# Layer 0's experts: the ScalarE gates of a block declared independent of the VectorE products of the same block

## The chip, the cores and the metric

The kernel runs on one core of a Trainium2 chip. The metric is the device time of one execution in microseconds (us), and the median of several runs is compared. Five engines work side by side, each through its own queue of instructions in order: PE (TensorE, matrix products; PEld is its loading of stationary operands), DVE (VectorE, elementwise work and reductions), ACT (ScalarE, activation functions), POOL (GpSimd, here mostly the issue of indirect transfers) and SP (SyncE, which issues the other transfers). A wait at the head of a queue holds all that stands behind it.

## The reference, cut to what matters

The program is a stack of four layers, each of attention followed by a mixture of experts, on `x` of 4 x 512 tokens with 128 features. The change lies in layer 0's experts, which compute for every token and expert

```python
h = jnp.einsum('td,edh->eth', xf, W0) + b0[:, None, :]
g = jax.nn.silu(jnp.einsum('td,edh->eth', xf, W1) + b1[:, None, :])
y = jnp.einsum('eth,ehd->etd', h * g, W2) + b2[:, None, :]
out = jnp.einsum('te,etd->td', combine.reshape(n * s, NUM_EXPERTS), y)
```

There are 8 experts with 512 hidden units, and `combine` is zero but for two experts of each token. In the code below `g` is "the gate" and `h * g` "the product".

## The kernel before, in words

The tokens are handled in two halves of 1024. `route` finds the two experts of each token and scatters the token's row into a buffer in DRAM, sorted by expert (`buf`, by POOL, L721). `experts` then works through 23 blocks of 128 sorted rows for each half of layer 0 (46 blocks), each with one expert's weights:

- `load` fetches four blocks' rows (L838, SP queue); `tokens` transposes them on PE (L848) and copies them out of PSUM.
- `up(j)` reads the expert's number, issues the load of 516 KB of weights `w` (L864, SP; three buffers) and does eight products on PE (L875) into `sc`, a PSUM tile of two banks with two buffers: the four gate chunks of 128 hidden units go to bank 1 first, and the four plain chunks to bank 0.
- `down(j)` goes over the four chunks. For each, ACT makes the gate `eg` from bank 1 (L890; four buffers), and DVE makes the product `hT` from bank 0 and the gate (L891; three buffers of four chunks). Both also read their biases from `w`, so that `w` is free for the load of block j + 3 only after the fourth product. Four products on PE follow (L902, into `av`), a copy `ys` on DVE (L910), and a store to `ybuf` (L911, SP). Two row transfers that are due, scatters or gathers, are issued on POOL behind each `ys` copy (`row_transfers`).

`down(j - 1)` is called after `up(j)`. When the first half's blocks are stored, `gather` fetches each token's two rows (`yg`, L935, POOL), two transfers behind each of the next eight `ys` copies, while the second half's blocks run; `combine` adds them to `x` on DVE (L953), and the statistics for the next layer's norm follow (L224, L226).

Nobody writes the order of layer 0 out by hand: a scheduler lays the instructions of each engine in an order that it finds with a timeline of its own, and then puts in the waits that the recorded dependencies need. Only the attention of layers 1 to 3 has a fixed order. The scheduler records a dependency between two instructions of different engines that touch the same tile in PSUM, also where both only read: so a gate of chunk `fc` on ACT waits for the product of chunk `fc - 1` on DVE, although the one reads bank 1 of `sc` and the other bank 0. The product needs the gate of its own chunk in any case.

Of the kernel before, what the change touches and what calls it, by code (L numbers as in the profile page):

```python
# [13 lines left out]
AF = mybir.ActivationFunctionType  # L14
ALU = mybir.AluOpType
# [4 lines left out]
P = 128  # L20
# [26 lines left out]
def tile_xattn_moe_stack(ctx: ExitStack, tc: tile.TileContext, a: dict, out: bass.AP):  # L47
# [10 lines left out]
    nc = tc.nc  # L58
# [13 lines left out]
    def ps_sc():  # L72
        return ps2.tile([P, 2, 512], F32, tag="sc", name="sc")

    def ps_tr():
        return ps2.tile([P, 512], F32, tag="tr", name="tr")

    def ps_av():
        return ps2.tile([P, 512], F32, tag="av", name="av")
# [3 lines left out]
    def evac(o, i, scale=None):  # L83

        turn[0] += 1
        if turn[0] % 2:
            if scale is None:
                nc.vector.tensor_copy(o, i)
            else:
                nc.vector.tensor_scalar(o, i, scale, None, ALU.mult)  # L90
        elif scale is None:
            nc.scalar.copy(o, i)
        else:
            nc.scalar.activation(o, i, AF.Copy, scale=scale)
# [545 lines left out]
    def row_transfers(n=2 * NH, behind=None):  # L640

        for start in rows_due[:n]:
            ins = start()
            if behind is not None:
                wait_for(ins, (behind,), "spread over the work beside it")
        del rows_due[:n]
# [161 lines left out]
    def wait_for(ins, others, why):  # L808
        for other in others:
            tc.add_manual_dep(  # L810
                ins.ins,
                other.ins.name,
                mybir.DependencyInfo(mybir.DependencyClass.Sync, mybir.DependencyReason.DATA),
                reason=why,
            )
# [8 lines left out]
    def experts(layer, half, routed, w2):  # L824

        ebs, _, scatters = routed
        nj, nf, nu = BLK[layer == 1], NF[layer], UPS[layer]
        pack = a[f"up{layer}"]
        width = pack.shape[2]
        bias = nu * nf * P  # L830
        loaded, toks = {}, {}

        def load(g):
            m = min(4, nj - 4 * g)
            if m <= 0:
                return
            tok = wff.tile([P, 4, D], F32, tag="tok", name="tok", bufs=2)
            get = nc.sync.dma_start(  # L838
                tok[:, 0:m, :], buf[half][4 * g * P : (4 * g + m) * P, :].rearrange("(c p) d -> p c d", p=P)
            )  # L840
            wait_for(get, scatters, "any token may lie in these blocks")
            loaded[g] = m, tok

        def tokens(g):
            m, tok = loaded.pop(g)
            q = ps_tr()
            for c in range(m):
                nc.tensor.transpose(q[:, c * P : (c + 1) * P], tok[:, c, :], ident)  # L848
            tokT = wff.tile([P, 4 * P], F32, tag="tokT", name="tokT", bufs=2)
            evac(tokT[:, 0 : m * P], q[:, 0 : m * P])  # L850
            toks[g] = tokT

        def up(j):

            xT = toks[j // 4][:, (j % 4) * P : (j % 4 + 1) * P]
            e = nc.values_load(
                ebs[0:1, j : j + 1],
                engines=[mybir.EngineType.SP, mybir.EngineType.PE],
                min_val=0,
                max_val=E - 1,  # L860
                skip_runtime_bounds_check_because="a count of at most E - 1, by a minimum",
            )
            w = wff.tile([P, 1032], F32, tag="w", name="w")
            nc.sync.dma_start(w[:, 0:width], pack[bass.ds(e, 1), :, :].rearrange("o p n -> p (o n)"))  # L864
            sc = ps_sc()
            for u in reversed(range(nu)):
                for fc in range(nf):
                    at = (u * nf + fc) * P
                    if layer == 0:
                        dst = sc[:, u, fc * P : (fc + 1) * P]  # L870
                    elif layer == 3:
                        dst = sc[:, fc // 2, fc % 2 * P : (fc % 2 + 1) * P]
                    else:
                        dst = sc[:, 0, fc * P : (fc + 1) * P]
                    nc.tensor.matmul(dst, w[:, at : at + P], xT, start=True, stop=True)  # L875
            return e, w, sc

        stores = []

        def down(j, e, w, sc):  # L880
            hT = p3.tile([P, nf, P], F32, tag="hT", name="hT")
            if layer == 2:
                nc.scalar.activation(hT.rearrange("p f t -> p (f t)"), sc[:, 0, 0 : nf * P], AF.Gelu)
            for fc in range(nf if layer != 2 else 0):
                up = sc[:, 0, fc * P : (fc + 1) * P]
                b0 = w[:, bias + fc : bias + fc + 1]
                if layer == 0:
                    g = p2.tile([P, P], F32, tag="eg", name="eg", bufs=4)
                    b1 = w[:, bias + nf + fc : bias + nf + fc + 1]
                    nc.scalar.activation(g, sc[:, 1, fc * P : (fc + 1) * P], AF.Silu, bias=b1)  # L890
                    nc.vector.scalar_tensor_tensor(hT[:, fc, :], up, b0, g, ALU.add, ALU.mult)  # L891
                elif layer == 1:
                    nc.scalar.activation(hT[:, fc, :], up, AF.Gelu, bias=b0)
                else:
                    up = sc[:, fc // 2, fc % 2 * P : (fc % 2 + 1) * P]
                    if fc < 2:
                        nc.vector.tensor_scalar(hT[:, fc, :], up, b0, 0.0, ALU.add, ALU.max)
                    else:
                        nc.scalar.activation(hT[:, fc, :], up, AF.Relu, bias=b0)
            y = ps_av()  # L900
            for fc in range(nf):
                nc.tensor.matmul(  # L902
                    y[:, 0:D],
                    hT[:, fc, :],
                    w2[:, bass.ds(e, 1), fc, :].rearrange("p o d -> p (o d)"),
                    start=(fc == 0),
                    stop=(fc == nf - 1),
                )
            ys = p3.tile([P, D], F32, tag="ys", name="ys")
            row_transfers(2, nc.vector.tensor_copy(ys, y[:, 0:D]))  # L910
            stores.append(nc.sync.dma_start(ybuf[half][j * P : (j + 1) * P, :], ys))  # L911


        load(0)
        load(1)
        tokens(0)
        last = None
        for j in range(nj):
            this = (j, *up(j))
            if last:  # L920
                down(*last)
            last = this
            if j % 4 == 2 and j // 4 + 1 in loaded:
                tokens(j // 4 + 1)
                load(j // 4 + 2)
            yield
        down(*last)
        return stores

# [288 lines left out]
    gates = []  # L1218
# [176 lines left out]
```

## Time and profile before

| | us |
|---|---|
| median of three runs | 1413.1 (1406.45 to 1416.71) |
| the profiled execution | 1326.58 |
| its span, first to last instruction | 1324.7 |
| layer 0's first `up` product to its last gate | 117.85 to 293.66 |

So the profiled execution is 86.5 us shorter than the median, and 1.9 us of it lie around the span. Its mean granted TensorE clock was 0.93 of full speed; for the other runs no clock is known. The second section of the page slices the span in forty pieces of 33.1 us; layer 0's blocks fill the slices four to nine:

```profile
PE   4885897897777778988999999857899999899881
...
PEclk8786998998899889989999999988999999999996
...
GB/s 220 0 61 98 163 225 179 171 156 80 26 9 37 38 62 50 151 148 93 42 38 46 49 50 102 127 144 140 132 62 34 50 34 33 83 91 163 202 184 57
```

A digit is a busy share in tenths; GB/s is what the DMA engines moved in each slice. The two groups of instructions that the change touches, from the fifth section (count, busy time, mean ns of one, and the idle time of the engine just before them):

```profile
L890 ACT ACTIVATE eg<-sc,w 128x128 f32<-128x128 f32 x184 | 66.2, 367 | 98.5 <-DVE hT L891 72.7
...
L891 DVE SCALAR_TENSOR_TENSOR hT<-sc,w,eg 128x128 f32<-128x128 f32 x184 | 63.0, 348 | 55.1 <-ACT eg L890 52.7
```

### The profile page before, as it was taken

Reading aid. Unit: us, or ns where it says so; the run is one execution under the profiler, and the core shown is the slowest. Engines: PE = TensorE matmul, PEld = TensorE weight load, DVE = VectorE, ACT = ScalarE, POOL = GpSimd, SP = SyncE. Lnnn points to the kernel's source line nnn. Section 1 sums busy time; section 2 is a strip of 40 time slices with the busy share of each in tenths; the row PEclk is TensorE's granted clock in tenths of the full one; section 3 lists DMA queues with packets and bytes.
Section 4 is the critical chain, followed back from the end, with each engine's and each line's share of the span. In section 5 each row is a group of like instructions: output and inputs, shape, how many; then the busy total and the mean of one; then the engine's idle time right before and its main releaser. Section 6 shows DMA issues by size and latency. Waiting matters only on the chain.

```text
span 1324.7 us, 26947 instructions
## 1 busy us (share of the span) xinstructions
PE 1099.2 (83%) x9435; PEld 904.1 (68%) x9435; DVE 748.5 (57%) x2057; ACT 588.2 (44%) x2290; POOL 252.4 (19%) x281
## 2 busy tenths in 40 slices
PE   4885897897777778988999999857899999899881
PEld 3774887773343445877787778746778887789781
DVE  5572554656767566433666766424376676646452
ACT  1112443355444444536556655322565665533230
POOL 2023122204000020221000004045030000403424
PEclk8786998998899889989999999988999999999996
DMA  7013575552101121553112223444421211335762
GB/s 220 0 61 98 163 225 179 171 156 80 26 9 37 38 62 50 151 148 93 42 38 46 49 50 102 127 144 140 132 62 34 50 34 33 83 91 163 202 184 57
DMA packets 136996, 126.82 MB, mean 96 GB/s; under 512 B 13466, under 2 KB 116511, under 8 KB 136479
## 3 DMA queue, kind: packets, MB, share of 16 engines
q1 hardware_dynamic: 129695, 110.39, 30.0%
q0 software_dynamic: 7168, 14.69, 3.8%
q8 instruction: 78, 1.28, 0.4%
q14 instruction: 55, 0.45, 0.1%
HBM read 101.31 MB, written 23.72 MB: 94 GB/s over the span
## 4 chain that ended last, share of the span: by engine, by line
PE 38%; DVE 7%; DMA 6%; ACT 3%; issue 3%; POOL 2%; SPq 1%; POOLq 0%; DVEq 0%; ACTq 0%
PE sc L608 5%; PE sc L875 5%; PE tr L368 5%; PE tr L422 4%; PE av L405 4%; PE av L902 4%; DMA w<-in_up 4%; PE sc L593 2%; PE av L387 2%; ACT probs L305 2%; DVE nm L291 2%; POOL yg L935 1%; PE sc L557 1%; PE tr L848 1%; DVE aT L412 1%
## 5 line engine op out<-in xcount | busy, mean ns | idle before, releaser
L305 ACT ACTIVATE probs<-sc,nm 128x154 f32<-128x154 f32 x768 | 286.3, 402 | 169.1 <-DVE nm L291 169.0
L875 PE MATMUL sc<-tokT,w 128*128 128x128 f32 x1528 | 210.8, 287 | 32.8 <-DMA w<-in_up 26.7
L875 PEld LDWEIGHTS sc<-tokT,w 128*128 128x128 f32 x1528 | 189.7, 198 | 46.6 <-DMA w<-in_up 13.0
L291 DVE TENSOR_REDUCE nm<-sc 128x6 f32<-128x924 f32 x144 | 143.2, 1011 | 86.6 <-PE sc L608 50.7
L902 PE MATMUL av<-w,hT 128*128 x1160 | 173.4, 284 | 10.1 <-DVE hT L891 7.3
L305 ACT ACTIVATION_READ_ACCUMULATOR probs<-sc,nm 128x1 f32 x768 | 168.2, 219 | 0.0
L902 PEld LDWEIGHTS av<-w,hT 128*128 128x128 f32 x1160 | 149.9, 195 | 21.2 <-DVE hT L891 11.4
L935 POOL DMA_INDIRECT yg<-ybuf,su x112 | 106.7, 953 | 275.6 <-DVE pT L261 63.7
L233 POOL TENSOR_TENSOR rstd<-ve,nhalf 128x4 f32<-128x4 f32 x32 | 33.2, 1039 | 619.4 <-DVE ve L231 499.2
L721 POOL DMA_INDIRECT buf<-xn,su x112 | 108.1, 965 | 171.3 <-DVE hT L891 43.7
L261 DVE COPY pT<-tr 128x512 f32<-128x512 f32 x160 | 107.4, 688 | 49.2 <-PE tr L368 43.9
L368 PE MATMUL tr<-ident,probs 128*128 128x128 f32 x768 | 121.5, 289 | 0.8 <-DVE rT L334 0.6
L405 PE MATMUL av<-pT,vm 128*64 128x128 f32 (+1 forms) x1536 | 102.7, 284 | 8.8 <-DVE pT L261 8.7
L890 ACT ACTIVATE eg<-sc,w 128x128 f32<-128x128 f32 x184 | 66.2, 367 | 98.5 <-DVE hT L891 72.7
L368 PEld LDWEIGHTS tr<-ident,probs 128*128 128x128 f32 x768 | 86.0, 145 | 28.8 <-issue 12.7
L891 DVE SCALAR_TENSOR_TENSOR hT<-sc,w,eg 128x128 f32<-128x128 f32 x184 | 63.0, 348 | 55.1 <-ACT eg L890 52.7
L910 DVE COPY ys<-av 128x128 f32<-128x128 f32 x168 | 48.5, 289 | 78.7 <-PE av L902 73.3
L405 PEld LDWEIGHTS av<-pT,vm 128*64 128x64 f32 (+1 forms) x1536 | 65.3, 127 | 35.6 <-issue 18.2
L608 PE MATMUL sc<-kT,qT 64*128 64x154 f32 x1024 | 86.5, 308 | 3.5 <-ACT probs L305 3.5
L608 PEld LDWEIGHTS sc<-kT,qT 64*128 64x128 f32 x1024 | 71.0, 189 | 14.3 <-issue 9.7
L593 PE MATMUL sc<-xnT,wq 128*128 128x128 f32 x512 | 67.1, 286 | 2.9 <-ACT probs L305 2.9
L422 PE MATMUL tr<-wo,aT 128*128 128x128 f32 x512 | 66.1, 284 | 1.6 <-DVE xnT L253 1.3
(252 smaller groups left out, 1477.7 us busy)
## 6 DMA issues: line engine op xcount, KB each, us to landing
w<-in_up SPq DMA_DIRECT2D x46, 516.0 KB
w<-in_up SPq DMA_DIRECT2D x76, 258.0 KB
rep<-rd SPq DMA_DIRECT2D x64, 256.0 KB
ybuf<-ys SPq DMA_DIRECT2D x168, 64.0 KB
tok<-buf SPq DMA_DIRECT2D x36, 256.0 KB
w<-in_down SPq DMA_DIRECT2D x3, 2048.0 KB
w<-in_up SPq DMA_DIRECT2D x46, 128.0 KB
buf<-zero SPq DMA_DIRECT2D x2, 1472.0 KB
```

The lines of the kernel that those rows point to most:

```text
L261: return nc.vector.tensor_copy(o, i)
L291: nc.vector.tensor_reduce(self.at.heads(self.nm, g, n), self.sc[g][:, :, 0 : n * S2].rearrange("p j (s k) -> p j s k", s=n), AX.X, ALU.max ...
L305: nc.scalar.activation(self.pr[:, h, :], self.sc[g][:, j, s * S2 : (s + 1) * S2], AF.Exp, bias=self.nm[:, h : h + 1], accum_out=self.rs[:, ...
L368: nc.tensor.transpose(q[:, t * P : (t + 1) * P], self.pr[:, h, 0:P], ident)
L405: nc.tensor.matmul(av[rows, cols], v, self.pT[n][:, t, :], start=False, stop=last)
L422: nc.tensor.matmul(o[:, 0:D], self.aT[:, c, :], self.at.wo[:, c, :], start=(c == 0), stop=(c == self.nb - 1))
L593: nc.tensor.matmul(sc[:, c // 4, c % 4 * P : (c % 4 + 1) * P], wq[:, c * P : (c + 1) * P], at.xnT[:, i * P : (i + 1) * P], start=True, sto ...
L608: nc.tensor.matmul(sc[:, j, s * S2 : (s + 1) * S2], at.qT[i][rows, c, :], at.kT[rows, c, :], start=True, stop=True)
L721: ins = nc.gpsimd.indirect_dma_start(out=buf[half], out_offset=bass.IndirectOffsetOnAxis(ap=su[:, t : t + 1], axis=0), in_=xns[t // NI][:, ...
L875: nc.tensor.matmul(dst, w[:, at : at + P], xT, start=True, stop=True)
L902: nc.tensor.matmul(y[:, 0:D], hT[:, fc, :], w2[:, bass.ds(e, 1), fc, :].rearrange("p o d -> p (o d)"), start=(fc == 0), stop=(fc == nf - 1),)
L935: ins = nc.gpsimd.indirect_dma_start(out=yg[:, t, :], out_offset=None, in_=ybuf[half], in_offset=bass.IndirectOffsetOnAxis(ap=su[:, t : t ...
```

## The change

The products of a block are collected in a list, and each gate is declared independent of all products of its own block that come before it. Nothing is computed in another way, and no instruction is added or taken away.

```diff
         def down(j, e, w, sc):
             hT = p3.tile([P, nf, P], F32, tag="hT", name="hT")
+            products = []
...
                 if layer == 0:
                     g = p2.tile([P, P], F32, tag="eg", name="eg", bufs=4)
                     b1 = w[:, bias + nf + fc : bias + nf + fc + 1]
-                    nc.scalar.activation(g, sc[:, 1, fc * P : (fc + 1) * P], AF.Silu, bias=b1)
-                    nc.vector.scalar_tensor_tensor(hT[:, fc, :], up, b0, g, ALU.add, ALU.mult)
+                    silu = nc.scalar.activation(g, sc[:, 1, fc * P : (fc + 1) * P], AF.Silu, bias=b1)
+
+                    for other in products:
+                        tc.declare_no_dep(silu.ins, other.ins, reason="distinct banks and gates")
+                    products.append(nc.vector.scalar_tensor_tensor(hT[:, fc, :], up, b0, g, ALU.add, ALU.mult))
```

The scheduler sees other dependencies and so lays out another order. Both programs hold the same instructions on every engine. Their orders agree from the start of the program to layer 0's first blocks, and again from the start of layer 1's attention on, but for one exchange of two neighbours on DVE and one read of an expert's number that stands a few instructions further ahead on PE; in layer 0's experts they differ on all five engines. Write gate j, product j, `ys` j, D j (the four products of L902) and U j (the eight of L875) for block j, counted from 0. On DVE the order around one block in the second half's gather was and is

```text
before:  ys 23, product 24 b c d, product 25 a, combine 1a, ys 24, product 25 b, combine 1b, ...
after:   ys 23, product 24 c d, product 25 a b, ys 24, product 25 c d, combine 1a 1b, ..., product 26 a b, ys 25, ...
```

where the gathers of pair 1 (a and b: the rows of a token's two experts) are issued behind `ys` 23, those of pair 2 behind `ys` 24, and so on. On POOL one `pow` of the norm (L233) is two gathers later than it was. On PE, U j + 1 stands ahead of D j in both, and the transposes of L848 and of the route stand elsewhere among them. On SP, weight load j stands behind the store of block j - 4 before, and behind that of block j - 4 or j - 5 now.

## The prediction

> **What bounds the kernel now.** I read the busy shares of the page first, then the stretches of layer 0's experts with the busy time of each engine, then the waits inside that stage, and last the instructions in order of time.
>
> ```profile
> PE 1099.2 (83%) x9435; PEld 904.1 (68%) x9435; DVE 748.5 (57%) x2057; ACT 588.2 (44%) x2290; POOL 252.4 (19%) x281
> ```
>
> PE leads over the whole span, so ACT and DVE, the two engines that the change sets free of each other, matter only where PE waits for them. The stretches of the stage (us and count of PE, PEld, DVE, ACT and POOL, then PE's granted clock, DMA share and GB/s):
>
> ```profile
> 118.00:150.00 32.00, 28.17 (x230) 27.20 (x231) 17.46 (x74) 15.60 (x35) 0.00 (x0) 0.93 0.53 156
> 150.00:187.00 37.00, 35.60 (x287) 34.00 (x287) 19.94 (x58) 17.23 (x47) 15.38 (x16) 0.97 0.65 195
> 187.00:220.00 33.00, 26.24 (x215) 24.60 (x215) 15.18 (x47) 12.35 (x35) 3.94 (x4) 1.00 0.65 199
> 220.00:250.00 30.00, 25.25 (x171) 22.75 (x172) 17.48 (x65) 9.32 (x26) 12.61 (x13) 0.89 0.54 159
> 250.00:294.00 44.00, 40.62 (x318) 36.57 (x316) 24.45 (x75) 20.49 (x56) 1.04 (x1) 1.00 0.55 166
> ```
>
> PE is busy for 155.9 of 176 us. So 20.1 us of idle PE is nearly all that any change of this stage can win, plus what a slowed clock cost: it was 0.89 in the fourth stretch, and 0.66 in 222 to 232 us. The waits of the stage (total us, times, longest):
>
> ```profile
> ACT eg L890 <- DVE hT L891: 72.7, 130, 4.1
> DVE hT L891 <- ACT eg L890: 52.7, 97, 4.3
> ...
> DVE x L953 <- DMA yg<-ybuf,su: 11.6, 10, 3.3
> ...
> PE sc L875 <- DMA w<-in_up: 8.5, 7, 2.6
> ...
> PE av L902 <- DVE hT L891: 7.3, 11, 2.0
> ```
>
> The two largest are the ping-pong that the change cuts, 125 us; PE's own, 8.5 and 7.3 us, are small. In order of time a block of the second stretch reads (start, us, then what it waited for):
>
> ```profile
> 158.65 0.37 ACT L890 ACTIVATE eg<-sc,w 128x128 f32<-128x128 f32 x1 [0.42 <-DVE hT L891]
> 159.05 0.35 DVE L891 SCALAR_TENSOR_TENSOR hT<-sc,w,eg 128x128 f32<-128x128 f32 x1 [0.43 <-ACT eg L890]
> ...
> 159.44 0.37 ACT L890 ACTIVATE eg<-sc,w 128x128 f32<-128x128 f32 x1 [0.42 <-DVE hT L891]
> 159.79 0.97 PEld L902 LDWEIGHTS av<-w,hT 128*128 128x128 f32 x8
> ...
> 161.42 1.86 PEld L875 LDWEIGHTS sc<-tokT,w 128*128 128x128 f32 x16 [0.66 <-ACT eg L890]
> 161.45 2.02 PE L875 MATMUL sc<-tokT,w 128*128 128x128 f32 x16 [0.49 <-DMA w<-in_up]
> ```
>
> Gates follow each other at 0.79 us, one product in between. A block has three such steps and then about 0.4 us, as the next block's first gate waits for no product: 2.8 us. PE needs 1.86 + 0.97 us for U and D and 0.12 us for transposes (four in 0.47 us, every fourth block): 2.95 us. The ping-pong is thus no longer than PE's own block; it costs only because it ends late, and holds the release of `w` with it.
>
> In the second half's gather another chain rules (DVE and POOL alone):
>
> ```profile
> 213.09 0.35 DVE L891 SCALAR_TENSOR_TENSOR hT<-sc,w,eg 128x128 f32<-128x128 f32 x1 [0.38 <-ACT eg L890]
> 216.72 0.35 DVE L953 SCALAR_TENSOR_TENSOR x<-yg,wa,x 128x128 f32<-128x128 f32 x1 [3.28 <-DMA yg<-ybuf,su]
> 216.99 0.28 DVE L910 COPY ys<-av 128x128 f32<-128x128 f32 x1
> ...
> 223.38 0.35 DVE L953 SCALAR_TENSOR_TENSOR x<-yg,wb,x 128x128 f32<-128x128 f32 x1 [2.67 <-DMA yg<-ybuf,su]
> ```
> ```profile
> 217.54 1.06 POOL L935 DMA_INDIRECT yg<-ybuf,su  x1 [3.02 <-DVE hT L891]
> 218.91 0.94 POOL L935 DMA_INDIRECT yg<-ybuf,su  x1 [0.30 <-issue]
> ```
>
> A `ys` copy releases two gathers, DVE stops at the combine of these rows, and the next `ys` stands behind it: one trip of a gather for each block.
>
> **The Trainium skill.** PSUM — Partial Sum Buffer, section "PSUM bank collisions raise a hardware error", says that two engines must be kept apart by bank and quadrant, reads against reads included, and that other banks run clean. Gates and products read different banks, so running them together should cost neither of them time; nothing in this trace shows a collision. The same page, "Engine vs sequencer instructions", calls the queues of ScalarE and VectorE strict FIFO: the trace agrees, the combine's 3.28 us hold products that could have run. TensorE: Matmul & The Clock Gate, section "What's actually happening", says that the clock is halved after an idle window of about 3.4 us; the trace agrees roughly: sixteen products from 226.21 us on, after PE gaps of 1.4 and 2.0 us at 217.6 and 224.1, took 3.68 us and not 1.95.
>
> **The change part by part.** I cut the stage by the starts of `ys` copies: `ys` 0 at 126.22, 7 at 155.24, 16 at 184.57, 23 at 210.44, 32 at 251.74, 45 at 294.99 us.
>
> *Ping-pong.* 138 waits of a gate go. A gate still waits for the product that used its buffer four gates earlier, in the block before, normally long done. Two gates in a row took 0.62 to 0.87 us, so four take 1.2 to 1.6 us, and the fourth product ends some 1.8 us after U j, not 3.1. The time on ACT and DVE is hidden by PE's 2.95 us and gives nothing; what counts is the next item.
>
> *Weight loads.* Load j + 3 goes out with product j, now 1.3 us sooner. One load took 3.9 us (issued 157.50, U at 161.45), beside a token load 5.7 us (141.95 to 147.66). From product j (1.8 us after U j) to U j + 3 lie three D and two U less 1.8: 3 x 0.97 + 2 x 1.87 - 1.8 = 4.85 us. So the usual load is hidden, and one beside tokens is late by up to 0.9 us. SP's queue doesn't hold them: the store ahead of load j + 3 is that of block j - 1 or older, whose `ys` comes before product j.
>
> *126 to 155:* 29.0 us. PE needs 7 x 2.95 and 3.4 for the route's products, 24.1. The route's table loads on ACT (1.28 + 0.2 + 1.28) remain, now after gate 4 and not after gate 3a. The 2.62 us for `w` at 147.66 go, with the slow clock behind it: **3** of 4.9.
>
> *155 to 185:* 29.3 us against 9 x 2.95 + 1.9 = 28.5: **0.5**. The route's slots are ready at product 8 and not 4 of DVE, but the scatters stay behind `ys` 7 to 14: nothing.
>
> *185 to 210:* 25.9 us against 20.7. PE waited 1.55 and 2.40 us for `w` where token loads crowd (DMA share 0.94 in 187 to 192). These loads stay: **2.5**, bounds 0 and 4.
>
> *210 to 252:* 41.3 us for nine blocks, 4.6 each, against 26.6. Now the `ys` of the next block stands ahead of the combine, so two blocks share one trip: 0.55 us to the first gather, 1.37 to the second, which lands after 2.9 (median; 4.5 longest), then about 1.9 us of combine, statistics, two products and waits to the second `ys` after it: 6.7 to 8.3 us for two blocks, 3.4 to 4.2 each. Nine blocks take 30 to 37 us. I take 33.3: **8**, bounds 4 and 11. DVE still stops at combines, but with products already handed over. The `pow` that moves past two gathers on POOL costs nothing: its norm is due blocks later.
>
> *252 to 295:* 43.3 us against 13 x 2.95 and 3.3 for attention's first products, 41.7: **1**.
>
> The sum is 15 us, bounds 4 and 22 (no more than PE's idle time and its slow clock hold): 1326.6 - 15 = 1311.6 in an execution like the profiled one. The median of 1413.1 is 86.5 us above it; with a slower PE the ping-pong matters less and the gather's trip the same. I take the same 15 us off: **1398**.
>
> **The rivals.** *PE hides it* (0.37): the second and fifth stretch have PE busy 96 and 92%, and loads and gathers take the place of the ping-pong: only half of each entry comes, 4 to 12 us, 1401 to 1409. Against it: in 210 to 252 PE isn't the bound. That a gate still waits for products through its four buffers, so that the change does little, belongs here, with 0 us at the least.
>
> *Late weights make it slower* (0.07): U j + 3 waits for its load at every block, as blocks come faster and loads crowd each other. The gain is lost when loads land on average 0.5 us after they are due (15 + 8.5 us, over 46 blocks), so at 5.4 us against 4.85; at 5.8 us, 20 us more are lost, 1433. For it: 5.7 us beside tokens. Against: 3.9 us at 222 GB/s, and the DMA engines reached 290.
>
> **How the numbers follow.** Gain as summed, 12 to 22 us: 0.56. Hidden by PE: 0.37. Slower: 0.07. The range takes the bounds 4 and 22 and the spread of a median (the three runs span 10 us): 1386 to 1412. One per cent is 14 us, about what a measurement of this kernel can tell from no change: faster by more 0.50, which is the summed case but for its lowest part, within 0.44, slower 0.06.
>
> **What will show it.** The waits of gates for products fall from 72.7 to under 15 us; `w` waits of PE from 8.5 to under 4; `ys` 23 to 32 from 41.3 to 30 to 37 us; `ys` 0 to 45 from 168.8 to some 154; everything after layer 0 as before. PE still waiting 8 us or more for `w`, or nine blocks still at 41, would prove me wrong.

## The result

| | median | runs |
|---|---|---|
| before | 1409.82 us | four, 1406.45 to 1416.71 |
| after | 1390.56 us | four, 1383.12 to 1395.60 |

The ratio is 0.9863 with a 95% interval of 0.9833 to 0.9893: 19.3 us less, between 15.1 and 23.5. The profiled execution of after took 1392.88 us, one of these four; that of before took 1326.58. The runs come from chips of two speeds: in other comparisons below the kernel before took 1321.9 and 1326.5 us, at a granted clock of 0.92 to 0.94, where the four runs of after here show 0.90 to 0.92; so only stretches of the stage are compared across chips, and medians within one comparison.

### The profile page after: what moved, and what is told of

Its sections match the earlier page's. It is cut to its first block, busy times and chain, and to the rows that moved or that the text cites. A ratio compares the mean times of both kernels' runs of the same rounds, so it can differ in the third digit from the quotient of the medians.

```text
span 1390.8 us, 26946 instructions
## 1 busy us (share of the span) xinstructions
PE 1125.7 (81%) x9435; PEld 924.2 (66%) x9435; DVE 736.2 (53%) x2057; ACT 575.6 (41%) x2290; POOL 252.9 (18%) x281
## 4 chain that ended last, share of the span: by engine, by line
PE 36%; DVE 8%; issue 4%; ACT 4%; DMA 4%; another core or an unknown queue 3%; POOL 1%; SPq 1%; POOLq 0%; DVEq 0%; ACTq 0%
PE sc L875 5%; PE sc L608 5%; PE av L405 4%; PE av L906 4%; PE tr L368 4%; PE tr L422 4%; DMA w<-in_up 3%; ACT probs L305 2%; PE sc L593 2%; PE av L387 2%; DVE nm L291 2%; PE sc L557 1%; POOL yg L939 1%; DVE aT L412 1%
## 5 line engine op out<-in xcount | busy, mean ns | idle before, releaser
L875 PE MATMUL sc<-tokT,w 128*128 128x128 f32 x1528 | 214.6, 290 | 19.8 <-DMA w<-in_up 14.8
L875 PEld LDWEIGHTS sc<-tokT,w 128*128 128x128 f32 x1528 | 195.0, 202 | 31.0 <-DMA w<-in_up 11.1
L906 PE MATMUL av<-w,hT 128*128 x1160 | 179.2, 292 | 42.7 <-issue 19.2
L906 PEld LDWEIGHTS av<-w,hT 128*128 128x128 f32 x1160 | 155.9, 201 | 53.9 <-issue 22.9
L233 POOL TENSOR_TENSOR rstd<-ve,nhalf 128x4 f32<-128x4 f32 x32 | 33.1, 1034 | 652.4 <-DVE ve L231 544.4
L891 ACT ACTIVATE eg<-sc,w 128x128 f32<-128x128 f32 x184 | 52.9, 370 | 89.2 <-PE sc L875 52.2
L895 DVE SCALAR_TENSOR_TENSOR hT<-sc,w,eg 128x128 f32<-128x128 f32 x184 | 55.9, 342 | 53.4 <-ACT eg L891 50.6
L593 PE MATMUL sc<-xnT,wq 128*128 128x128 f32 x512 | 70.8, 296 | 2.9 <-ACT probs L305 2.9
L593 PEld LDWEIGHTS sc<-xnT,wq 128*128 128x128 f32 x512 | 64.9, 206 | 8.2 <-issue 4.3
```

The costliest lines, as they stand in the source:

```text
L593: nc.tensor.matmul(sc[:, c // 4, c % 4 * P : (c % 4 + 1) * P], wq[:, c * P : (c + 1) * P], at.xnT[:, i * P : (i + 1) * P], start=True, sto ...
L895: products.append(nc.vector.scalar_tensor_tensor(hT[:, fc, :], up, b0, g, ALU.add, ALU.mult))
L906: nc.tensor.matmul(y[:, 0:D], hT[:, fc, :], w2[:, bass.ds(e, 1), fc, :].rearrange("p o d -> p (o d)"), start=(fc == 0), stop=(fc == nf - 1),)
```

## The profile after

The two groups of the change, from the page (gates are now L891, products L895):

```profile
L891 ACT ACTIVATE eg<-sc,w 128x128 f32<-128x128 f32 x184 | 52.9, 370 | 89.2 <-PE sc L875 52.2
...
L895 DVE SCALAR_TENSOR_TENSOR hT<-sc,w,eg 128x128 f32<-128x128 f32 x184 | 55.9, 342 | 53.4 <-ACT eg L891 50.6
```

ACT still idles 89 us ahead of gates, but what ends the idle time is now PE's product and no longer DVE's: idle time of an engine that is ahead. The waits of the stage (total us, times, longest) say the same:

```profile
ACT eg L891 <- PE sc L875: 52.2, 32, 3.1
DVE hT L895 <- ACT eg L891: 50.6, 31, 4.3
...
DVE x L957 <- DMA yg<-ybuf,su: 8.7, 6, 3.4
...
ACT eg L891 <- DVE hT L895: 2.8, 2, 2.6
...
PE sc L875 <- DMA w<-in_up: 2.7, 5, 0.8
```

The 130 waits of gates for products have become two, and the 97 of products for gates 31, fewer than one for each of the 46 blocks. Gates wait for PE instead, 52.2 us where it was 24.2. Side by side with a product a gate takes 370 ns in the mean, and a product 342 (367 and 348 before): reading two banks of one tile together costs neither any time that shows. A block of the last stretch in order of time (start, us):

```profile
248.10 1.14 ACT L891 ACTIVATE eg<-sc,w 128x128 f32<-128x128 f32 x4 [0.82 <-PE sc L875]
...
248.81 1.86 PEld L875 LDWEIGHTS sc<-tokT,w 128*128 128x128 f32 x16
...
249.23 0.60 DVE L895 SCALAR_TENSOR_TENSOR hT<-sc,w,eg 128x128 f32<-128x128 f32 x2
...
250.59 0.97 PEld L906 LDWEIGHTS av<-w,hT 128*128 128x128 f32 x8
...
251.49 1.87 PEld L875 LDWEIGHTS sc<-tokT,w 128*128 128x128 f32 x16
```

Four gates in 1.14 us; the last product ends at 249.83, and D starts 0.76 us later, when PE comes to it. From U to U PE needs 2.68 us and stands still nowhere: it bounds this stretch. The two kernels by the starts of `ys` copies:

| `ys` | before, us | after, us | gain | forecast |
|---|---|---|---|---|
| 0 to 7 | 29.02 | 24.01 | 5.0 | 3 |
| 7 to 16 | 29.33 | 30.15 | -0.8 | 0.5 |
| 16 to 23 | 25.87 | 22.20 | 3.7 | 2.5 |
| 23 to 33 | 44.24 | 37.46 | 6.8 | 8 |
| 33 to 45 | 40.31 | 34.24 | 6.1 | 1 |
| 0 to 45 | 168.77 | 148.06 | 20.7 | 15 |

The cut here is at `ys` 33, where the prediction cut at 32: in after, `ys` 32 was held behind a combine until 238.47 and `ys` 33 came 0.72 us behind it. By the cut at 32 the two gains are 4.6 and 8.3, and part of what belongs to the gather is booked in the stretch behind it.

## The experiments

"Stage" is `ys` 0 to 45 of one profiled execution; times are medians against the kernel before in the same comparison.

### Where the gain lies: one half at a time

```diff
-                    for other in products:
+                    for other in products if half == 0 else ():
```

> The gates are declared independent only in the first half's 23 blocks; the second half keeps its waits. Measured for the whole change: ys 0 to 45 from 168.8 to 148.1 us, of which ys 0 to 23 gave 7.9 us. Theory A (each block gains by its own freed gates): ys 0 to 23 about 76 us (84.2 before), ys 23 to 45 as before, 84.6; time about 1402. Rival B (the gain comes from the second half's gather, where two blocks share one trip, and what ys 0 to 23 showed is chance between two executions): ys 0 to 23 about 84, time about 1410.

Measured: 1312.14 us against 1321.89, ratio 0.9927 (0.9905 to 0.9949). `ys` 0 to 23 took 73.2 us, 23 to 45 82.5.

With `half == 1` instead:

> The gates are declared independent only in the second half's 23 blocks. Theory A: ys 0 to 23 about 84 us as before, ys 23 to 45 about 72 (84.6 before, 71.7 with the whole change); time about 1397. Rival B: the same 72, but then the whole gain, time about 1391.

Measured: 1308.24 us, ratio 0.9888 (0.9817 to 0.9960). `ys` 0 to 23 took 82.0, 23 to 45 70.7. The absolute times expected were for the slower chip; the gains of the medians, 9.8 and 13.7 us, are near those of theory A (8 and 13), though the second interval is wide. Each half gains by its own gates, and B falls.

### Waits or order

`in_order` records a dependency between two instructions of DVE that costs no wait and only fixes which comes first.

```diff
+                    if fc == 1 and copies:
+                        in_order(products[1], copies[-1])
...
-            row_transfers(2, nc.vector.tensor_copy(ys, y[:, 0:D]))
+            copies.append(nc.vector.tensor_copy(ys, y[:, 0:D]))
+            row_transfers(2, copies[-1])
```

> The waits are gone as in the changed kernel, but an order without a wait puts each block's second product behind the ys copy of the block before, as it stood before the change; with it the scheduler puts combine 1a ahead of that ys again. Theory A (the waits themselves cost): ys 0 to 45 148 to 151 us, time 1391 to 1394. Rival B (the order of DVE around ys and combine costs): ys 23 to 33 goes back from 37.5 to about 44 us (the value before), the rest stays: ys 0 to 45 about 155, time about 1398.

Measured: 1303.63 us against 1321.89, ratio 0.9855 (0.9772 to 0.9938). The stage took 146.9 us, `ys` 23 to 33 37.2 and `ys` 33 to 45 33.9. In the last stretch DVE's order is that of the kernel before again from `ys` 35 on, but for one copy of tokens: one product of a block stands ahead of each `ys`, three behind it (products are L903 and `ys` L924):

```profile
258.67 0.35 DVE L903 SCALAR_TENSOR_TENSOR hT<-sc,w,eg 128x128 f32<-128x128 f32 x1 [1.12 <-ACT eg L899]
259.16 0.29 DVE L924 COPY ys<-av 128x128 f32<-128x128 f32 x1
259.37 0.86 DVE L903 SCALAR_TENSOR_TENSOR hT<-sc,w,eg 128x128 f32<-128x128 f32 x3
```

With this order and without the waits the stretch takes 33.9 us; with this order and the waits, before, it took 40.3. There the waits cost, not the order.

In the gather the old order came back only in part. The first combine of a pair stands ahead of its `ys` for five of the eight pairs; the second stands behind three products, where it was one or none. The 37.2 us are those of the changed kernel (37.5), so the order is not worth the 7 us of this stretch, where the prediction put its largest gain on it. A smaller share isn't excluded: e5_after_again, below, took 35.4 at the same granted clock of 1.00. DVE stood still at combines as long as before, 11.7 us in nine waits against 11.6 in ten. What differs is how it goes on afterwards. DVE in this kernel, from the first stop on:

```profile
203.60 0.35 DVE L903 SCALAR_TENSOR_TENSOR hT<-sc,w,eg 128x128 f32<-128x128 f32 x1 [1.12 <-ACT eg L899]
206.94 0.35 DVE L968 SCALAR_TENSOR_TENSOR x<-yg,wa,x 128x128 f32<-128x128 f32 x1 [3.00 <-DMA yg<-ybuf,su]
207.21 0.28 DVE L924 COPY ys<-av 128x128 f32<-128x128 f32 x1
207.41 0.86 DVE L903 SCALAR_TENSOR_TENSOR hT<-sc,w,eg 128x128 f32<-128x128 f32 x3
```

and ACT beside the same stop in the kernel before:

```profile
217.57 0.37 ACT L890 ACTIVATE eg<-sc,w 128x128 f32<-128x128 f32 x1 [3.73 <-DVE hT L891]
```

Here a stopped DVE stops ACT for 3.73 us too, and the block's last product ends at about 219.3, 2.0 us after the `ys` copy of 216.99 to 217.27. Without the waits the block's four gates were done by 204.34, long before the stop ended, and the last product ends 0.8 us after that copy (208.27 against 207.49).

### How many waits matter

Only the third gate of a block waits for a product (for the second):

```diff
-                    for other in products:
+                    for other in products if fc % 2 else ():
```

> Of a block's three waits of a gate for a product one is kept: that of the third gate for the second product. Theory A1 (the ping-pong costs only as far as a block's chain of gates and products is longer than PE's block of 2.7 to 2.8 us; with one wait it is about 2 us): ys 0 to 45 148 to 151 us, time 1391 to 1394. Rival A2 (each wait costs alike, through what it delays): a third of the gain is lost, ys 0 to 45 about 155 us, time about 1397.

Measured: 1302.34 us against 1321.89, ratio 0.9819 (0.9730 to 0.9909); stage 144.7 us, `ys` 33 to 45 34.9. One wait a block costs little: the runs without waits took 33.9 to 34.6 us there.

The second gate waits for the first product and the fourth for the third:

```diff
-                    for other in products:
+                    for other in products if fc == 2 else ():
```

> Two of a block's three waits are kept: those of the second gate for the first product and of the fourth for the third. A chain of gates and products is then about 2.5 us from its first gate to its last product, against 3.1 with three waits, 2.0 with one and 1.5 with none. Theory A1 (it costs as far as the chain, with the end of D and the next U that it lets start, is longer than PE's own 2.7 us a block: a threshold): ys 33 to 45 34.5 to 37 us, near the 34.3 without waits; ys 0 to 45 145 to 152. Rival A2' (a cost for each wait that only one kept wait escapes): two thirds of the way back, ys 33 to 45 38 to 39 us, ys 0 to 45 about 160.

Measured: 1399.95 us against 1408.04, ratio 0.9915 (0.9873 to 0.9956); stage 156.2, `ys` 33 to 45 37.4. This lies between the two theories: no sharp threshold, but no equal share for each wait either. Of the gain that the medians show without waits (19.3 us on such a chip) one wait less has brought 8.1.

All declarations kept, but one gate buffer:

```diff
-                    g = p2.tile([P, P], F32, tag="eg", name="eg", bufs=4)
+                    g = p2.tile([P, P], F32, tag="eg", name="eg", bufs=1)
```

> The declarations of the changed kernel, but one buffer for gates instead of four, so that each gate waits for the product before it through the buffer, the first gate of a block too: four waits a block, four times 0.79 = 3.16 us from a block's first gate to the next block's at the least. Theory A1: the whole gain is lost and some more, ys 33 to 45 41 to 44 us, ys 0 to 45 168 to 178, time 0 to 8 us over the kernel before. Rival C (the gain comes from the declaration's effect on the order, not from ACT running ahead of DVE): most of the gain stays, ys 0 to 45 under 155 us.

Measured: 1415.94 us against 1408.04, ratio 1.0048 (1.0025 to 1.0071); stage 174.3, `ys` 33 to 45 43.0. The declarations alone are worth nothing: what they let through, a wait through the buffer takes back, and 7.9 us more. This run doesn't part waits from order, though: in the last stretch the scheduler put one product ahead of each `ys` and three behind it again. What parts them is e3_oldorder. Together, `ys` 33 to 45 by the waits of a block (none: after, e2_half1, e3_oldorder, e5_after_again and e6_late; three: before, e1_half0 and e7_before_late; one profile each for the others):

| waits kept | 0 | 1 | 2 | 3 | 4 |
|---|---|---|---|---|---|
| us | 33.9 to 34.6 | 34.9 | 37.4 | 40.3 to 41.2 | 43.0 |

Nearly flat at first, then some 2 to 4 us for each. The chip's speed doesn't enter: the granted clock of this stretch was 1.00 in every profile. A place in the kernel before shows a loop that can bound it at three waits. From one block's last product to the last product two blocks on:

```profile
266.34 0.61 DVE L891 SCALAR_TENSOR_TENSOR hT<-sc,w,eg 128x128 f32<-128x128 f32 x2 [0.43 <-ACT eg L890]
266.74 0.30 PEld L902 LDWEIGHTS av<-w,hT 128*128 128x128 f32 x2 [0.49 <-DVE hT L891]
...
267.23 1.86 PEld L875 LDWEIGHTS sc<-tokT,w 128*128 128x128 f32 x16 [0.19 <-issue]
...
269.37 0.37 ACT L890 ACTIVATE eg<-sc,w 128x128 f32<-128x128 f32 x1 [0.36 <-PE sc L875]
...
272.49 0.35 DVE L891 SCALAR_TENSOR_TENSOR hT<-sc,w,eg 128x128 f32<-128x128 f32 x1 [0.44 <-ACT eg L890]
```

(The first row is that last product, to about 266.69, and the next block's first.) The last product lets the end of D start; U of the block two on stands behind it on PE; its first gate waits for the whole of U, and the chain of four gates and products follows, to 272.84: 6.15 us for two blocks, 3.08 each, against 2.68 that PE needs. The mean agrees: `ys` 36 to 45 took 3.08 us a block before (3.18 and 3.19 in e1_half0 and e7_before_late) and 2.71 in the changed kernel.

An estimate from these figures says what each wait does. Gates are 0.79 us apart with a wait and (1.14 - 0.37) / 3 = 0.26 without, so a wait less shortens the loop by 0.53 us, 0.26 a block: from 3.08 to 2.82 with two waits and 2.55 with one, which is under PE's 2.68. Measured were 2.89 and 2.75 us a block. So the loop can explain why the first wait is nearly free and the later ones are not; that it is this loop alone is not shown. Of the 6.1 us between the two kernels in `ys` 33 to 45, 3.3 lie in these nine blocks. The other 2.8 lie in the three blocks ahead of them, among attention's first products, and stay open.

### Is the gain tied to the chip, and is it lost later?

> The changed kernel once more, on the chip of these runs, where the kernel before took 1321.9 and not 1410 us. If what it saves is time in which PE stands still for waits (all theories but one), it saves the same microseconds: 18 to 21, ys 0 to 45 146 to 149 us. If it had saved slowed clock, it would save less here, where the granted clock is higher: under 12.

Measured: 1304.25 us against 1326.52, ratio 0.9822 (0.9750 to 0.9895), and 22.3 us less by the medians; the stage took 142.1 us, shorter than expected. The gain isn't smaller at the higher clock, as a gain of slowed clock would be. But part of the 26.7 us by which the stage is shorter than in the profile of before can be clock: in `ys` 0 to 7 and 23 to 33 it was 0.94 and 0.92 there and 1.00 here, at most 29.0 x 0.06 + 44.2 x 0.08 = 5.3 us by an estimate from these. After layer 0 no gain is seen to be lost. From `ys` 45 to the end the kernel before took 1029.7 us and this run 1034.7, both at a clock of 0.94; the six other profiles at this speed took 1022.0 to 1036.1, so 5 us say nothing. In the first profile of after this stretch took 1117.4 us at a clock of 0.91, and in e8_two_waits and e9_one_gate_buffer 1114.5 and 1112.2: that is the chip.

### What is left: the stops at combines

```diff
-                combine(0, k, i, routed[0], got)
+                combine(0, k, i, routed[0], got, copies[k * NI + i + 2] if layer == 0 else None)
...
-            nc.vector.scalar_tensor_tensor(xi, yg[:, t, :], cw[:, t : t + 1], xi, ALU.mult, ALU.add)
+            ins = nc.vector.scalar_tensor_tensor(xi, yg[:, t, :], cw[:, t : t + 1], xi, ALU.mult, ALU.add)
+            if behind is not None:
+                in_order(ins, behind)
```

> The changed kernel, with an order without a wait that puts each combine of the first half's rows behind the ys copy of one block later (combine 0 behind ys 25 and not ys 24, and so on). Theory A (DVE's stops at combines, 8.7 us in the changed kernel, are what keeps ys 23 to 33 above PE's own 10 x 2.8 = 28 us): the stops fall under 3 us, ys 23 to 33 from 37.5 to 29 to 32 us, the time 5 to 8 us under the changed kernel. Rival B (the stops are hidden, as the next blocks' products are handed over before them, and PE or the weights rule): ys 23 to 33 stays at 35 to 37.5, time as the changed kernel.

Measured: 1295.68 us (1292.38 to 1298.58) against 1304.25 (1301.41 to 1313.60) of the changed kernel and 1326.52 of before in the same comparison; ratio to before 0.9736 (0.9675 to 0.9797). The stops fell to 3.9 us (11.2 in e5_after_again), and `ys` 23 to 33 took 31.8. This is the best version, 31 us under the kernel before and 8.6 under the changed one, with no overlap of their runs.

The same later combines in the kernel before, waits kept:

> The kernel before, its waits kept, with the same later combines. Theory A (a combine that waits stops DVE, and through the kept waits ACT with it): the stops go, ys 23 to 33 from 44.2 to about 34 us (ten blocks at the 3.4 us that the ping-pong takes in ys 33 to 45), the rest as before: time about 9 us under the kernel before, and 3 to 4 us over e6_late in this stretch. Rival B (one trip of a gather for each block, wherever the combine stands): 42 to 44 us.

Measured: 1316.63 us against 1326.52, ratio 0.9930 (0.9902 to 0.9957); `ys` 23 to 33 took 35.3. No combine waited any more (`ys` is L921, the combine L965):

```profile
211.62 0.29 DVE L921 COPY ys<-av 128x128 f32<-128x128 f32 x1 [0.32 <-PE av L913]
211.83 0.34 DVE L965 SCALAR_TENSOR_TENSOR x<-yg,wa,x 128x128 f32<-128x128 f32 x1
```

Rival B, one trip of a gather for each block, falls. In `ys` 23 to 33, freed gates take 44.2 to 37.5 us, later combines 44.2 to 35.3, both 31.8: 6.8 and 8.9 singly, 12.5 together. Freed gates gain 6.8 us where DVE stops and 3.6 (35.3 to 31.8) where it hardly does. The difference of 3.2 us goes through the stops, as with the waits a stop also costs the gates that aren't made meanwhile; it is 1.5 us at the least by an estimate, as the clocks were 0.92 (before), 0.95 (after) and 1.00 (the other two), which can make 1.7 us of the 6.8. The rest is there without stops, as in the last stretch.

## Why the prediction was right, and where it was not

The median of after, 1390.6, lies 7.4 us under the 1398 forecast and in the range; 3.3 us of these are the median of before, 1409.8 here and 1413.1 there, and 4.3 the gain. Point by point, with the means over the profiled executions that kept all three waits in a stretch (before, e1_half0, e2_half1, and e7_before_late except in the gather, each where it applies) and those that kept none (after, e1_half0, e2_half1, e3_oldorder, e5_after_again, and e6_late except in the gather):

| `ys` | kept | freed | gain |
|---|---|---|---|
| 0 to 7 | 27.2 | 24.0 | 3.2 |
| 7 to 16 | 29.6 | 28.4 | 1.2 |
| 16 to 23 | 26.4 | 22.0 | 4.4 |
| 23 to 33 | 42.8 | 36.5 | 6.3 |
| 33 to 45 | 40.8 | 34.2 | 6.6 |

- **Ping-pong.** Under 15 us of gates' waits for products were forecast: 2.8 remain. Four gates were to take 1.2 to 1.6 us: 1.14.
- **Weight loads.** 8.5 us of PE's waits were to fall under 4: 2.7, and 1.8 in e5_after_again, though 5.0 in e3_oldorder. Late weights as a rival are gone; in no run with freed gates did these waits grow.
- **126 to 155 and 155 to 185.** 3 and 0.5 forecast, 3.2 and 1.2 in the means (2.3 and not 3.2 if the profile of before, whose clock was 0.94 there, is left out); the -0.8 of the first pair of profiles is the spread of single executions (27.6 to 30.2 us without waits).
- **185 to 210.** 2.5 forecast, 4.4 in the mean, just over the bound of 4. The step "these loads stay" was wrong: the waits for `w` of 1.55 and 2.40 us beside the token loads went with the rest; in the profile of after none is longer than 0.8.
- **210 to 252.** By the forecast's own cut the stretch took 36.7 us, within 30 to 37 but at its edge, and 4.6 us were gained of 8. The step behind it was wrong: "the `ys` of the next block stands ahead of the combine, so two blocks share one trip". e3_oldorder puts `ys` behind the combine again for five of eight pairs and keeps the gain. An order can gain here, as e7_before_late does with combines one block later, but the order that came with the change isn't what did. The gain came from gates made while DVE stood still (1.5 to 3.2 us, by the estimate above) and from what freed gates gain without stops.
- **252 to 295.** 1 us forecast, 8.3 by its own cut and 6.6 in the mean from `ys` 33 on. The step that failed is PE's need of 41.7 us, in three terms. "PE needs 1.86 + 0.97 us for U and D" sums the durations of two groups of weight loads, but a group's row reaches to the end of its last load, and the next group's first load starts before that. The trace of before shows it, in a place where PE happened not to wait:

```profile
169.33 1.87 PEld L875 LDWEIGHTS sc<-tokT,w 128*128 128x128 f32 x16
171.11 0.97 PEld L902 LDWEIGHTS av<-w,hT 128*128 128x128 f32 x8
172.01 1.87 PEld L875 LDWEIGHTS sc<-tokT,w 128*128 128x128 f32 x16
```

From start to start 172.01 - 169.33 = 2.68, where the two sum to 2.83: 0.15 us too much a block, 2.0 in 13. And behind the last block no U follows. The weight loads of U and D in this stretch, before (counts, busy us, mean ns, then idle us of the loads ahead of them):

```profile
L875 PEld LDWEIGHTS sc<-tokT,w 128*128 128x128 f32 x192 | 22.4, 192 | 3.9 <-DVE hT L891 1.3 <-ACT eg L890 1.3 <-issue 0.7
L902 PEld LDWEIGHTS av<-w,hT 128*128 128x128 f32 x104 | 13.4, 191 | 2.8 <-DVE hT L891 2.1 <-issue 0.5
```

At 16 loads for each U and 8 for each D that is 12 U for 13 D, so one U of 1.87 us too many was counted. Nor are there any transposes: the last of L848 starts at 240.0 us, and the forecast had 13 x 0.12 = 1.6 us of them here. Without the three the need is 36.3 us against 43.3, room for 7.0 where the forecast saw 1.6; and where no combine held `ys` 32 back, in e3_oldorder and e6_late, the stretch took 36.6 and 36.4. The idle time is in the rows: 6.7 us ahead of U and D, most of it ended by products and gates, and 1.7 in after (from `ys` 32 on). So "the ping-pong is thus no longer than PE's own block" was wrong too: at 3.08 us against 2.68 it was longer here.

- **The sum.** 15 us; the medians gained 19.3, and 22.3 on the faster chip. By the cuts of the forecast the first pair of profiles has 3.4 us less than forecast in the gather and 7.3 more in the last stretch. That the two partly cancel is luck: the total was near, the places were not. Taking the same microseconds off at another speed held.
- **The rivals.** "PE hides it" rested on PE's busy shares of 96 and 92%, and these say less than they seem to. In `ys` 33 to 45 PE counts as busy for 37.2 us before (290 products) and 34.2 after (288), for the same twelve blocks: a row in which PE starts and stops among late products counts as longer (the last D before, with such a stop, for 1.53 us, others for 1.06). So the 20.1 us of idle PE were no good limit for the whole stage either: in `ys` 0 to 45 PE counts as busy for 148.5 us before and 136.2 in e5_after_again, and the clock accounts for at most the 5.3 us above. The Trainium skill, Perfetto Trace Analysis, section "Identifying the Most-Contended Engine", says that the busy share of matmuls is no good measure of the distance from PE's limit, and to use that of the weight loads. The trace agrees: PEld was busy 33.3 of 40.3 us, 83%, before and 32.3 of 34.2, 94%, after. By that row there was room in the last stretch.

## What to carry to other kernels

Read what an engine needs for a step from start to start in a place where it doesn't wait, and not as a sum of group durations or from a busy share; count, too, which steps a stretch really holds. Here 41.7 us for a need of 36.3 hid a gain. A wait between two engines costs more when one of them stops for something else, as the other can't work ahead: 3.73 us of ACT behind one stop of DVE. And taking out some of a chain's waits can be enough: here it was two of three in the last stretch, 34.9 us where none left takes 34.2 and three take 40.3.

## What was not expected of the hardware

Gates 0.79 us apart in the ping-pong follow each other at 0.26 us when nothing stands between: four took 1.14 us, of 0.37 each alone, and three products 0.86, of 0.35 each. The Trainium skill, Perfetto Trace Analysis, section "Optimizing Scalar/DVE Operations", says that part of an instruction's profiled time, the acknowledgement of its write, overlaps with the next instruction. The rows agree in size, 0.37 - 0.26 and 0.35 - 0.26, some 0.1 us on both engines; that it is the acknowledgement no run here shows. In the ping-pong no two gates stand in a row, so this overlap is lost at each step: 0.79 us against 0.26, where the single durations of a gate and a product sum to 0.72.
